# The two-dimensional convolution and whitening kernel: samples of the last two channel groups packed in halves, last-pass loads and covariances one group sooner, and a last pass with full-width evictions, another output layout and stores on two queues

## The chip, the cores and the metric

The kernel runs on one core of one Trainium2 chip. The metric is the device time of one execution in microseconds. Times of before: 909.0 us, the median of three runs (908.66 to 910.16). Engines are named as in the profile: PE (TensorE), DVE (VectorE), ACT (ScalarE), POOL (GpSimd) and SP (SyncE, which issues DMAs).

## The reference

The input is x with shape (4, 64, 256, 256), float32. Layer 0 is a long convolution in two dimensions, computed in the reference by FFTs, whose filter for each channel is a product of a row filter and a column filter. Layer 1 subtracts a mean and whitens the 64 channels.

```python
hx = _implicit_filter(z, Xw1, ...); hy = _implicit_filter(z, Yw1, ...)   # (1, 256, 64)
k = einsum('ijk,imk->ijmk', hx, hy)[0]          # rank one for each channel
y = irfft2(rfft2(x) * rfft2(k) / fft_size)[..., :256, :256] + x * bias[:, None, None]
x1 = transpose(y, (1, 0, 2, 3)).reshape(64, -1)
x1_s = x1[:, ::9]                               # every ninth pixel
mean1 = mean(x1_s); cov = x1_s @ x1_s.T / n + 0.01 * I
out = isqrt_newton_schulz(cov, 5) @ (x1 - mean1)
```

The whitening matrix needs the sampled pixels of all channels and all images, so no output can be written before the whole convolution is done.

## The kernel before, in words

**Start.** Small networks give the filters' taps, which go through DRAM (`g_d`) and come back as Toeplitz matrices (`toep`), one set for each group of 8 channels. Between the small products `busy(n)` issues n plain 128x128 matmuls whose result nobody reads. The last such call is `busy(16)`, ahead of the first half group.

**Main loop.** A step is one channel group g (8 channels, `CG`) of one image n; 32 steps, `steps`. Groups 0 to 5 run over all four images; the last 8 steps alternate groups 6 and 7 for each image, so that an image is complete after every second step. In a step c goes 0, 2, 4, 6. Each `group(first, second)` does the first product for two channels of `first` and, in the same PE sequence, the second product for two channels two positions back in the order (`second`); ACT copies the first product from PSUM to `o1`, DVE adds the bias term to the second product and writes it over x (line 406). Eight PSUM banks turn over, four for each `group`. The order of PE, SP, DVE, ACT and POOL is the program's order (`tc.manual_schedule`), up to the last pass, whose order the tile scheduler sets.

**Packing.** The covariance needs every ninth pixel. `pack_ops` gives 9 DVE operations (`copy_predicated`, line 318) for each step; they copy candidates into `samp[n]`. `store` puts them in the list `todo` when the last pair of channels of a step is stored, and `pack(time)` issues operations until a budget of cost units is used: `pack(2.5)` in each `group`, ahead of `store`. In the last step only the first four channels go this way (9 smaller operations); the others are packed by PE (`pack_by_pe`, line 299).

**Covariance.** `covariance(n)` is 116 small matmuls on `samp[n]` (line 332). For images 0 to 2 it stands in the step of group 7 of the next image, at c == 4; for image 3 after the loop. Then `samp[n]` is free.

**Loads of the last pass.** The convolved images lie in DRAM as `y_d[n]`. A piece is 128 rows (two halves of the image for each of 64 channels) by 4096 pixels, 2 MB; there are 32. `homes` lists 13 buffers that are taken over from the convolution: `e` scratch, `t` Toeplitz sets, `s` sample tiles, `i` x tiles. `early` says after which (step, c) a piece is loaded ahead; nine are. The other four follow after the loop; each waits until its buffer is free. From the 14th piece on, a load waits until the piece 13 places earlier has been stored. All of these loads are issued by SP (line 356).

**Whitening.** `whitening` is a chain of 64x64 products on PE and small DVE and ACT operations, with `spin(n)` (n plain matmuls) between them. It ends with `W` and `shift`.

**Last pass.** For each piece, four times, over 1024 columns: eight matmuls (line 622; each float32 product shows as two matmuls) into two PSUM banks, then two ACT and two DVE operations on 64 partitions by 512 columns each (lines 627 and 630), which add the shift and write over the piece. POOL issues the stores (line 635): whole pieces, and quarters for the first two and the last two pieces.

Of the kernel before, what the change touches and what calls it, by code (L numbers as in the profile page):

```python
# [34 lines left out]
F32 = mybir.dt.float32  # L38
I32 = mybir.dt.int32
AF = mybir.ActivationFunctionType  # L40
ALU = mybir.AluOpType
# [22 lines left out]
def conv_whiten_kernel(ctx: ExitStack, tc: tile.TileContext, a: dict, out: bass.AP):  # L64
# [112 lines left out]
    nc.scalar.dma_start(out=g0_d[CG:], in_=taps[ORDER : ORDER + CG])  # L177
    nc.gpsimd.dma_start(out=g_d, in_=taps)
    nc.gpsimd.tensor_copy(rows, mask[:, NB - 1, 0, :])
    busy(16)  # L180

    def new_toeplitz(g):

# [142 lines left out]
    def covariance(n):  # L326
# [18 lines left out]

    homes = [
        {"t": (tpool, "toep"), "s": (spool, "samp"), "i": (xpool, "in"), "e": (epool, "extra")}[k]
        for k in "eetssiistiits"
    ]

    def load_y(i):
# [19 lines left out]
    for g in range(1, C // CG):  # L371
# [3 lines left out]
            blocks[k // 4, k % 4 * 2] = (g, part)  # L375

    early = {
        (26, 4): 1, (27, 0): 1, (27, 4): 1, (28, 0): 1, (29, 6): 1, (30, 2): 1, (31, 2): 1, (31, 4): 1, (31, 6): 1
    }
    orders = [list(range(L // HP)), list(reversed(range(L // HP)))]  # L380

    def pack(time=math.inf):
        while todo and time > 0:
            cost, op = todo.pop(0)
            op()
            time -= cost

    def group(first, second):

        units = []  # L390
        g1, n1, c1, x1, o1s1 = first
        g2, n2, c2, x2, o1s2 = second
        for u in range(2):
            job2 = (bank(f"p2_{g2}_{n2}_{c2 + u}"), o1s2[u], toep[g2][:, 1, c2 + u, :])
            job1 = (bank(f"p1_{g1}_{n1}_{c1 + u}"), x1[:, c1 + u], toep[g1][:, 0, c1 + u, :])
            units.append((job1, job2))

        toeplitz_products(units, orders[0])
        orders.reverse()
        for u in range(2):  # L400
            o1 = o1pool.tile([P, H2, L], F32, tag="o1", name=f"o1_{g1}_{n1}_{c1 + u}")
            for to, fr in ((slice(0, HP), slice(HP, P)), (slice(HP, P), slice(0, HP))):
                nc.scalar.copy(o1[to], units[u][0][0][fr])  # L403
            o1s1.append(o1)
            ch = g2 * CG + c2 + u
            nc.vector.scalar_tensor_tensor(  # L406
                x2[:, c2 + u], x2[:, c2 + u], bias[:, ch : ch + 1], units[u][1][0],
                ALU.mult, ALU.add,
            )

        pack(2.5)
        store(second)

    def store(second):
        g, n, c, yt, _ = second
        last = (g, n) == steps[-1]
        for b in range(H2):
            row = b * C + g * CG + c
            nc.sync.dma_start(
                out=y_d[n][row : row + 2, :].rearrange("c (p w) -> p c w", w=L),  # L420
                in_=yt[:, c : c + 2, b],
            )
        if last and c == CG // 2 - 2 or not last and c == CG - 2:
            todo.extend(pack_ops(g, n, yt, slice(0, c + 2)))

    spins = []

# [23 lines left out]
    def whitening(i15, ones):  # L451
# [57 lines left out]
        for k in range(1, N_ITER - 1):  # L509
            pq = product(T, T, f"pq{k}")  # L510
            if before is not None:
                next_z(k - 1, before)
            spin(1)
            Q = Qs[k % 2]
            nc.vector.tensor_copy(Q, pq)
            pm = product(Q, M, f"pm_{k}")
            before = T
            if k == 1:
                nc.vector.scalar_tensor_tensor(Z[:, 0:C], Ah, rn_c, one_i15, ALU.mult, ALU.add)
                pzm = product(Z[:, 0:C], mean, "pzm")  # L520
                nc.scalar.copy(Z[:, C : C + 1], pzm)
            if k < N_ITER - 2:
                spin(1)
                T, M = Ts[k % 2], Ms[k % 2]
                nc.vector.scalar_tensor_tensor(T, pm, -0.5, one_i15, ALU.mult, ALU.add)
                nc.vector.tensor_copy(M, pm)
                for _ in range(2):
                    steps_rs.pop(0)()
            else:
                next_z(k, T)  # L530
                spin(1)

                T = place(2 * C, rows=C)
                nc.vector.scalar_tensor_tensor(
                    T.rearrange("p (u c) -> p u c", u=2),
                    pm.unsqueeze(1).to_broadcast([C, 2, C]), -0.5, i15, ALU.mult, ALU.add,
                )
        Z = Zs[(N_ITER - 2) % 2]
        pw = product(T, Z, "pw")
        W = place(C)  # L540
        nc.vector.tensor_scalar(W, pw[:, 0:C], rs, None, ALU.mult)
        shift = const.tile([P, 1], F32, tag="shift", name="shift")
# [4 lines left out]
    with tc.manual_schedule(  # L547
        engines={engines.PE, engines.SP, engines.DVE, engines.Activation, engines.Pool}
    ):
        toep = {0: new_toeplitz(0)}  # L550

        for f, lo, hi in ((0, 0, 2), (0, 2, 4), (0, 4, 6), (1, 0, 2), (0, 6, 8), (1, 2, 4), (1, 4, 8)):
            for half in range(2):
                load_toeplitz(toep[0], 0, f, half, lo, hi, nc.scalar if half else nc.sync)
        for c in range(0, CG, 2):
            load_x(x_tiles[1], *steps[1], c)
        for i, (g, n) in enumerate(steps):
            xt = x_tiles[i % 4]
            for c in range(0, CG, 2):
                item = (g, n, c, xt, [])  # L560
                if g == C // CG - 1 and n > 0 and c == 4:
                    covariance(n - 1)
                if len(pending) == 2:
                    group(item, pending.pop(0))
                else:
                    half_group(item, 0)
                pending.append(item)
                if i == 0 and c == 6:

                    fold = const.tile([P, C], F32, tag="fold", name="fold")  # L570
                    nc.vector.tensor_tensor(fold, ident[:, 0:C], ident[:, C:P], ALU.add)

                    nc.scalar.activation(bf[:, 0:1], samp[0][:, 0, 0, C : C + 1], AF.Sqrt)
                if i == 1 and c < CG - 2:
                    load_pick(c // 2 * 3, c // 2 * 3 + 3)

                if i + 2 < len(steps):
                    load_x(x_tiles[(i + 2) % 4], *steps[i + 2], c)
                if (i, c) in blocks:
                    tg, part = blocks[i, c]  # L580
                    if part == 0:
                        toep[tg] = new_toeplitz(tg)
                    lo = part % 2 * CG // 2
                    load_toeplitz(toep[tg], tg, part // 4, part // 2 % 2, lo, lo + CG // 2)
                for _ in range(early.get((i, c), 0)):
                    load_next()
        g, n, c, yt, _ = pending[0]
        for item in pending:
            half_group(item, 1)
            pack(1.0)  # L590
            store(item)

        pack()
        i15 = place(2 * C, rows=C).rearrange("p (u c) -> p u c", u=2)
        for u in range(2):
            nc.vector.tensor_scalar(i15[:, u], ident[0:C, 0:C], 1.5, None, ALU.mult)
        ones = place(P, rows=C)
        nc.gpsimd.memset(ones, 1.0)  # L598
        for lo in range(CG // 2, CG, 2):
            pack_by_pe(g, n, yt, slice(lo, lo + 2))  # L600
        covariance(NB - 1)
        while len(loaded) < len(homes):
            load_next()
        W, shift = whitening(i15, ones)


    halves = [slice(u * C, (u + 1) * C) for u in range(2)]
    for i, (n, q) in enumerate(pieces):
        yt = loaded.pop(i)
        o = out[n].rearrange("b c f -> (b c) f")[:, q * FP : (q + 1) * FP]  # L610

        part = FP if 1 < i < len(pieces) - 2 else FP // 4
        for w in range(FP // 1024):


            po = [
                psA.tile([P, 512], F32, tag="psA", name=f"po_{n}_{q}_{w}_{u}") for u in range(2)
            ]
            cols = [slice((2 * w + k) * 512, (2 * w + k + 1) * 512) for k in range(2)]
            for k in range(2):  # L620
                for u in range(2):
                    nc.tensor.matmul(  # L622
                        po[u][halves[k]], lhsT=W[halves[u]], rhs=yt[halves[u], cols[k]],
                        start=True, stop=True,
                    )
            for k in range(2):
                nc.scalar.activation(  # L627
                    yt[halves[0], cols[k]], po[0][halves[k]], AF.Identity, bias=shift[halves[k]]
                )
                nc.vector.tensor_scalar(  # L630
                    yt[halves[1], cols[k]], po[1][halves[k]], shift[halves[k]], None, ALU.add
                )
            end = (w + 1) * 1024
            if end % part == 0:
                nc.gpsimd.dma_start(out=o[:, end - part : end], in_=yt[:, end - part : end])  # L635
        if i + len(homes) < len(pieces):
            loaded[i + len(homes)] = load_y(i + len(homes))

# [57 lines left out]
```

## Time and profile before

| | before |
|---|---|
| median of three runs | 909.0 us (908.66 to 910.16) |
| profiled execution, its own time | 907.37 us |
| its span | 905.3 us |
| PE busy | 784.6 us (87%) |
| DVE busy | 656.2 us (72%) |
| ACT busy | 481.5 us (53%) |
| DMA, mean | 285.61 MB, 315 GB/s |
| HBM read, written | 149.35 MB, 134.44 MB |
| line 630, DVE, 64x512 | 256 of 750 ns |
| line 627, ACT, 64x512 | 256 of 683 ns |

The profile divides the span into 40 slices of 22.6 us. PE and its weight load are busy in all of them up to about 620 us; from there on the DMA share is full to nearly the end. The profiled execution took 907.37 us by its own clock, 2.1 us more than the span of its instructions.

### The profile page before, as it was taken

What the parts mean: (1) busy time and instruction counts of PE and PEld (TensorE: products, weight loads), DVE (VectorE), ACT (ScalarE), POOL (GpSimd) and SP (SyncE); (2) the same over time, 40 slices, a digit from 0 to 9 for tenths busy, and PEclk for the clock granted to TensorE, in tenths of its full rate; (3) what the DMA queues carried; (4) which work ended last, traced back from release to release, by engine and by line L of the source; (5) the groups of instructions that cost most, each with busy time, mean ns of one, the idle gap of its engine ahead of it and who ended that gap; (6) DMA issues with size and microseconds to landing.
All of it is one profiled execution on the core that took longest, in us unless ns stands there. A gap on an engine that the chain in (4) does not pass through costs nothing.

```text
span 905.3 us, 28200 instructions
## 1 busy us (share of the span) xinstructions
PE 784.6 (87%) x11892; PEld 630.5 (70%) x11892; DVE 656.2 (72%) x868; ACT 481.5 (53%) x804; POOL 26.4 (3%) x63
## 2 busy tenths in 40 slices
PE   8999999999999999999999999999977777765500
PEld 7999999999999999999999999998411111111100
DVE  3378777877687868776787766767799999996500
ACT  2655555545454545455555544541698888884400
POOL 1000000000000000000000000000100000000010
PEclk9999999999999999999999999999999999996655
DMA  7988779788788788888997899879999999999998
GB/s 215 317 256 263 247 244 273 249 264 247 255 269 262 239 260 270 260 248 256 291 283 233 292 389 341 289 245 384 382 389 428 430 433 429 429 430 431 433 429 340
DMA packets 117496, 285.61 MB, mean 315 GB/s; under 512 B 8987, under 2 KB 91212, under 8 KB 109692
## 3 DMA queue, kind: packets, MB, share of 16 engines
q1 hardware_dynamic: 109676, 215.58, 70.5%
q0 software_dynamic: 6400, 67.31, 17.6%
q8 instruction: 94, 1.54, 0.7%
q10 hardware_dynamic: 1296, 0.93, 0.5%
q14 instruction: 30, 0.25, 0.1%
HBM read 149.35 MB, written 134.44 MB: 313 GB/s over the span
## 4 chain that ended last, share of the span: by engine, by line
PE 68%; DVE 16%; issue 9%; DMA 5%; POOL 0%; ACT 0%; POOLq 0%; DVEq 0%; SPq 0%; ACTq 0%
PE p L219 63%; DVE yi L630 14%; DMA yi<-y_d 3%; PE pc L332 2%; DVE samp L318 1%; DMA out_dram<-yi 1%; PE ph L251 1%; PE po L622 1%; DMA toep<-g_d 0%; POOL out_dram L635 0%; DVE x L288 0%; DVE x L406 0%; ACT yi L627 0%; PE pm L157 0%; PE spin L433 0%
## 5 line engine op out<-in xcount | busy, mean ns | idle before, releaser
L219 PE MATMUL p<-toep,o 64*64 64x64 f32 (+3 forms) x5040 | 578.6, 284 | 0.0
L219 PE MATMUL p<-toep,x 64*64 64x64 f32 (+3 forms) x5040 | 578.4, 284 | 0.1
L219 PEld LDWEIGHTS p<-toep,x 64*128 64x128 f32 (+1 forms) x5040 | 534.6, 166 | 23.9 <-POOLq L235 0.4
L219 PEld LDWEIGHTS p<-toep,o 64*128 64x128 f32 (+1 forms) x5040 | 535.4, 166 | 10.4
L403 ACT COPY o<-p 64x512 f32<-64x512 f32 x504 | 292.2, 580 | 292.9 <-PE p L219 285.3
L318 DVE COPY_PREDICATED samp<-mask,x 128x448 f32<-128x448 int32 (+3 forms) x288 | 281.0, 976 | 6.7
L406 DVE SCALAR_TENSOR_TENSOR x<-x,bias,p 128x512 f32<-128x512 f32 x252 | 177.3, 743 | 138.6 <-PE p L219 138.2
L630 DVE TENSOR_SCALAR yi<-po,shift 64x512 f32<-64x512 f32 x256 | 192.1, 750 | 21.1 <-PE po L622 14.8
L622 PE MATMUL po<-yi,chain 64*64 64x512 f32 x1024 | 149.7, 652 | 61.7 <-DVE yi L630 42.2
L627 ACT ACTIVATE yi<-po,shift 64x512 f32<-64x512 f32 x256 | 174.7, 683 | 37.8 <-PE po L622 30.6
L622 PEld LDWEIGHTS po<-yi,chain 64*64 64x64 f32 x1024 | 34.9, 141 | 175.5 <-DVE yi L630 131.4
L635 POOL DMA_DIRECT2D out_dram<-yi x44 | 23.4, 533 | 254.5 <-DVE yi L630 132.4
L332 PE MATMUL pc<-samp 128*64 128x65 f32 x464 | 16.1, 233 | 2.2 <-ACT samp L308 2.2
L598 POOL MEMSET chain<- 64x128 f32 x1 | 0.2, 198 | 606.0 <-PE ph L251 606.0
L332 PEld LDWEIGHTS pc<-samp 128*64 128x64 f32 x464 | 15.5, 147 | 3.3 <-issue 3.3
L285 DVE COPY o<-ph 64x256 f32<-64x256 f32 x8 | 3.4, 422 | 11.2 <-PE ph L251 11.1
L340 DVE SCALAR_TENSOR_TENSOR cov<-pc,cov 128x65 f32<-128x65 f32 x4 | 0.9, 227 | 13.4 <-PE pc L332 13.4
L251 PE MATMUL ph<-toep,x 64*128 64x192 f32 (+3 forms) x64 | 8.0, 391 | 1.8 <-DMA toep<-g_d 1.8
L285 ACT COPY o<-ph 64x256 f32<-64x256 f32 x8 | 2.9, 366 | 12.1 <-PE ph L251 12.0
L251 PEld LDWEIGHTS ph<-toep,x 64*128 64x128 f32 x64 | 7.2, 234 | 2.5 <-issue 1.5
L299 PE MATMUL pk<-x,pick 128*128 128x56 f32 (+1 forms) x72 | 8.3, 292 | 0.0
L299 PEld LDWEIGHTS pk<-x,pick 128*128 128x128 f32 x72 | 8.1, 192 | 0.1
(93 smaller groups left out, 81.1 us busy)
## 6 DMA issues: line engine op xcount, KB each, us to landing
x<-in_x_dram SPq DMA_DIRECT2D x128, 512.0 KB, 5.5
y_d<-x SPq DMA_DIRECT2D x256, 256.0 KB, 4.0
yi<-y_d SPq DMA_DIRECT2D x32, 2048.0 KB, 14.7
out_dram<-yi POOLq DMA_DIRECT2D x28, 2048.0 KB, 42.8
out_dram<-yi POOLq DMA_DIRECT2D x16, 512.0 KB, 8.5
toep<-g_d SPq DMA_DIRECT2D x28, 256.0 KB, 6.1
toep<-g_d SPq DMA_DIRECT2D x29, 192.0 KB, 6.3
toep<-g_d SPq DMA_DIRECT2D x4, 128.0 KB, 4.0
```

The lines of the kernel that those rows point to most:

```text
L219: mm = nc.tensor.matmul(ps[q : q + w, m, HP * k : L], lhsT=src[parts, k // 2, m * P + q : m * P + q + w], rhs=t[parts, : stop : -1] if k e ...
L251: mm = nc.tensor.matmul(ps[m][:, HP * k : L], lhsT=src[parts, k // 2, m * P : (m + 1) * P], rhs=t[parts, : stop : -1] if k else t[parts, : ...
L285: copy(o1s[u][to, m], ps[fr])
L299: nc.tensor.matmul(pk[:, b, :, 0:nj], lhsT=pick[:, (s - b) % STEP, :], rhs=yt[:, cs, b, s : s + STEP * (nj - 1) + 1 : STEP], start=(s == 0 ...
L318: nc.vector.copy_predicated(dst, m, src)
L332: nc.tensor.matmul(pc[half], lhsT=samp[n][:, b, j, 0:C], rhs=samp[n][:, b, j, :], start=(b == 0 and j < 2), stop=(b == H2 - 1 and j >= NJ ...
L403: nc.scalar.copy(o1[to], units[u][0][0][fr])
L406: nc.vector.scalar_tensor_tensor(x2[:, c2 + u], x2[:, c2 + u], bias[:, ch : ch + 1], units[u][1][0], ALU.mult, ALU.add,)
L622: nc.tensor.matmul(po[u][halves[k]], lhsT=W[halves[u]], rhs=yt[halves[u], cols[k]], start=True, stop=True,)
L627: nc.scalar.activation(yt[halves[0], cols[k]], po[0][halves[k]], AF.Identity, bias=shift[halves[k]])
L630: nc.vector.tensor_scalar(yt[halves[1], cols[k]], po[1][halves[k]], shift[halves[k]], None, ALU.add)
L635: nc.gpsimd.dma_start(out=o[:, end - part : end], in_=yt[:, end - part : end])
```

## The change

The diff has these parts:

- **Start:** `busy(16)` becomes `busy(22)`.
- **Packing:** `store` comes ahead of `pack`, whose budget is now 2.92 units a group and is carried over in `credit`. For groups 6 and 7, in all images, a step's samples are packed in two halves of four channels (9 operations each); the first half is queued after the second pair of channels is stored.
- **Covariances:** those of images 0 to 2 at c == 2 instead of c == 4.
- **Loads ahead:** five of the nine entries of `early` come sooner, by two (one of them four) positions of c, and two entries of `homes` change places.
- **Whitening:** six `spin(1)` become `spin(2)`; `spin(4)` is added ahead of the last covariance and `spin(2)` after the last product; two small operations go from DVE to POOL.
- **Last pass:** ACT and DVE each do one operation on 128 partitions by 512 columns where they did two on 64. For that the output has another layout: the two 64-row halves of a result bank now hold pixels that lie half a piece apart, and a piece is one contiguous block of 2 MB in DRAM. Stores of piece 0 go in four parts, of pieces 1, 30 and 31 in two. SP issues the stores of piece 0 and of pieces 19 to 31; POOL those of pieces 1 to 18.

```diff
-    busy(16)
+    busy(22)
-        for k in "eetssiistiits"
+        for k in "eetssiistitis"
     early = {
-        (26, 4): 1, (27, 0): 1, (27, 4): 1, (28, 0): 1, (29, 6): 1, (30, 2): 1, (31, 2): 1, (31, 4): 1, (31, 6): 1
+        (26, 4): 1, (27, 0): 1, (27, 4): 1, (28, 0): 1, (29, 2): 1, (30, 0): 1, (31, 0): 1, (31, 2): 1, (31, 4): 1
     }
+    credit = [0.0]
     def pack(time=math.inf):
-        while todo and time > 0:
+        credit[0] += time
+        while todo and credit[0] > 0:
             cost, op = todo.pop(0)
             op()
-            time -= cost
+            credit[0] -= cost
+        if not todo:
+            credit[0] = min(credit[0], 0.0)
...
-        pack(2.5)
         store(second)
+        pack(2.92)
...
-        last = (g, n) == steps[-1]
+        halves = g >= C // CG - 2
-        if last and c == CG // 2 - 2 or not last and c == CG - 2:
-            todo.extend(pack_ops(g, n, yt, slice(0, c + 2)))
+        if c == CG - 2 and (g, n) != steps[-1]:
+            todo.extend(pack_ops(g, n, yt, slice(CG // 2 if halves else 0, CG)))
+        elif c == CG // 2 - 2 and halves:
+            todo.extend(pack_ops(g, n, yt, slice(0, CG // 2)))
...
-            spin(1)
+            spin(2)
...
         pw = product(T, Z, "pw")
+        spin(2)
...
-                if g == C // CG - 1 and n > 0 and c == 4:
+                if g == C // CG - 1 and n > 0 and c == 2:
                     covariance(n - 1)
...
-            nc.vector.tensor_scalar(i15[:, u], ident[0:C, 0:C], 1.5, None, ALU.mult)
+            nc.gpsimd.tensor_scalar(i15[:, u], ident[0:C, 0:C], 1.5, None, ALU.mult)
...
+        spin(4)
         covariance(NB - 1)
...
-        o = out[n].rearrange("b c f -> (b c) f")[:, q * FP : (q + 1) * FP]
-        part = FP if 1 < i < len(pieces) - 2 else FP // 4
+        v = yt.rearrange("p (v f) -> p v f", v=2)
+        o = out[n, q].rearrange("p (v f) -> p v f", v=2)
+        part = 512 if i == 0 else 1024 if i == 1 or i > len(pieces) - 3 else 2048
         for w in range(FP // 1024):
+            cols = slice(w * 512, (w + 1) * 512)
...
-                        po[u][halves[k]], lhsT=W[halves[u]], rhs=yt[halves[u], cols[k]],
+                        po[u][halves[k]], lhsT=W[halves[u]], rhs=v[halves[u], k, cols],
...
-            for k in range(2):
-                nc.scalar.activation(
-                    yt[halves[0], cols[k]], po[0][halves[k]], AF.Identity, bias=shift[halves[k]]
-                )
-                nc.vector.tensor_scalar(
-                    yt[halves[1], cols[k]], po[1][halves[k]], shift[halves[k]], None, ALU.add
-                )
-            end = (w + 1) * 1024
+            nc.scalar.activation(v[:, 0, cols], po[0], AF.Identity, bias=shift)
+            nc.vector.tensor_scalar(v[:, 1, cols], po[1], shift, None, ALU.add)
+            end = (w + 1) * 512
             if end % part == 0:
-                nc.gpsimd.dma_start(out=o[:, end - part : end], in_=yt[:, end - part : end])
+                issue = nc.sync if i == 0 or i + len(homes) >= len(pieces) else nc.gpsimd
+                issue.dma_start(out=o[:, :, end - part : end], in_=v[:, :, end - part : end])
...
-    out = nc.dram_tensor("out_0_dram", (NB, H2, C, PIX // H2), F32, kind="ExternalOutput").ap()
+    out = nc.dram_tensor("out_0_dram", (NB, PIX // H2 // FP, P, FP), F32, kind="ExternalOutput").ap()
```

More of the change, by code (lines that the diff above doesn't have):

```diff
@@ L522, in whitening @@
             if k < N_ITER - 2:
-                spin(1)
+                spin(2)
                 T, M = Ts[k % 2], Ms[k % 2]
@@ L530, in whitening @@
                 next_z(k, T)
-                spin(1)
+                spin(2)
                 T = place(2 * C, rows=C)
@@ L539, in whitening @@
         pw = product(T, Z, "pw")
+        spin(2)
         W = place(C)
@@ L618, in conv_whiten_kernel @@
             ]
-            cols = [slice((2 * w + k) * 512, (2 * w + k + 1) * 512) for k in range(2)]
             for k in range(2):
@@ L692 @@
     r = run_bass_kernel_spmd(nc, [arrays], core_ids=[0])
-    y = np.asarray(r.results[0]["out_0_dram"]).reshape(NB, H2, C, PIX // H2)
-    return np.ascontiguousarray(y.transpose(0, 2, 1, 3)).reshape(NB, C, L, L)
+    y = np.asarray(r.results[0]["out_0_dram"]).reshape(NB, PIX // H2 // FP, H2, C, H2, FP // 2)
+    return np.ascontiguousarray(y.transpose(0, 3, 4, 1, 2, 5)).reshape(NB, C, L, L)
```

## The prediction

> **What bounds the kernel now.** I read the 40 slices first, because they show where the bound changes.
>
> ```profile
> DVE  3378777877687868776787766767799999996500
> PEclk9999999999999999999999999999999999996655
> DMA  7988779788788788888997899879999999999998
> GB/s 215 317 256 263 247 244 273 249 264 247 255 269 262 239 260 270 260 248 256 291 283 233 292 389 341 289 245 384 382 389 428 430 433 429 429 430 431 433 429 340
> ```
>
> Up to about 618 us (27 slices) PE is full and DMA is not. From there to the end DMA runs at about 430 GB/s. DVE's nines in the last pass mislead: at the end DVE falls to 0 and DMA goes on, so DVE is ahead of what bounds. The chain of waits names DVE line 630 because it follows the last work back through the stores. I therefore asked for windows around the end of the loop (columns: PE, PEld, DVE, ACT, POOL busy, PE clock, DMA share, GB/s):
>
> ```profile
> 595.00:600.00 5.00, 5.00 (x88) 4.47 (x80) 4.93 (x7) 3.36 (x7) 0.00 (x0) 1.00 0.36 117
> 620.00:645.00 25.00, 21.36 (x251) 18.19 (x254) 14.08 (x46) 3.18 (x15) 0.00 (x0) 0.93 1.01 422
> 645.00:670.00 25.00, 21.47 (x150) 5.39 (x142) 24.23 (x34) 24.31 (x37) 5.00 (x10) 1.00 0.95 371
> 670.00:890.00 220.00, 126.36 (x866) 28.81 (x862) 167.25 (x223) 149.78 (x220) 17.37 (x33) 0.86 1.01 428
> ```
>
> From 670 to 890 nothing can be gained by engines: 428 GB/s in every stretch, reads and writes mixed. There are two soft places: the dips between 645 and 670, and idle DMA in the loop, where too few loads are queued. So the time is: first store, plus the bytes left then over 428 GB/s, plus what DMA loses to gaps. In the order of time, PE ahead of the first store and POOL from it on (start, duration, in brackets the idle time before):
>
> ```profile
> 618.27 8.28 PE L299 MATMUL pk<-x,pick 128*128 128x58 f32 x72
> 628.71 4.93 PE L332 MATMUL pc<-samp 128*64 128x65 f32 x116 [2.16 <-ACT samp L308]
> 643.16 7.47 PE L622 MATMUL po<-yi,chain 64*64 64x512 f32 x57 [0.38 <-DVE chain L541]
> ```
>
> ```profile
> 646.53 0.53 POOL L635 DMA_DIRECT2D out_dram<-yi  x1 [28.36 <-DVE yi L630]
> 663.61 0.53 POOL L635 DMA_DIRECT2D out_dram<-yi  x1 [5.66 <-DVE yi L630]
> 669.79 0.53 POOL L635 DMA_DIRECT2D out_dram<-yi  x1 [5.66 <-ACT yi L627]
> ```
>
> The covariance waits 2.16 us for a copy that waits for DVE's packing (ten operations, 621.21 to 628.07). Whole pieces reach POOL every 6.19 us, 2.1 MB each: 339 GB/s. Until loads come back, that is less than DMA can move; this makes the dips. Last the start of the kernel:
>
> ```profile
> 13.60:17.00 3.40, 1.65 (x11) 1.31 (x13) 0.00 (x0) 0.00 (x0) 0.00 (x0) 1.00 0.89 217
> 17.00:20.40 3.40, 3.40 (x27) 3.35 (x25) 0.46 (x2) 0.66 (x2) 0.00 (x0) 0.50 0.99 213
> ```
>
> PE waits for the first Toeplitz sets 1.33 and 0.45 us; in the next 3.4 us its clock is halved.
>
> **Start, busy(22).** Six more matmuls are 12 records; 32 of them took 3.74 us, so +1.4 us, from 13.58 to about 14.95, where the first half group begins anyway (14.91). They fill the 1.33 us wait. If then the half clock (17.0 to 20.4) goes, PE does in 1.7 us what took 3.4; no wait is recorded in that stretch, and the sets land ahead. I take -1.5 us, bounds 0 (the 0.45 us wait alone still halves it) and -1.7. The loop is PE-bound, so all later times move with it.
>
> **Packing in halves.** Groups 6 and 7 cost DVE 18 operations a step for 9. The rows:
>
> ```profile
> L318 DVE COPY_PREDICATED samp<-mask,x 128x448 f32<-128x448 int32 x155 | 150.9, 973 | 4.2
> L318 DVE COPY_PREDICATED samp<-mask,x 128x224 f32<-128x224 int32 x5 | 3.1, 611 | 0.2
> L406 DVE SCALAR_TENSOR_TENSOR x<-x,bias,p 128x512 f32<-128x512 f32 x252 | 177.3, 743 | 138.6 <-PE p L219 138.2
> ```
>
> A group then has 4.5 operations of 0.62 us and two of line 406, 1.40 us in the timeline together: 4.2 us. Stores of successive groups leave SP at 608.98 and 613.36, 4.4 us apart. So it fits by 0.2 us, and three covariances (3.71 us of PE each) give DVE slack. I cost it at nothing; the cover is PE, and PSUM banks are reused only a group later. Above 0.66 us for a half the group would be DVE-bound, and above 0.75 (17.5 us of four groups, plus 1.6 of covariances, less 5.6, over 18) their slack would be used up too; that is a rival below. The 2.92 budget in groups 0 to 5 leaves three full operations a group as now, at nothing.
>
> **End of the loop.** By the order of instructions DVE has seven half operations left after its last line 288 where it had ten: 4.5 us, done near 625, before PE's packing ends (626.55). The copy then ends near 627.0 and `spin(4)` (8 records; 14 took 1.83 us) at 627.65: the covariance starts 1.06 us sooner. PE has no gap, so I expect no half clock from 628: 3.71 us as in the loop (599.27) for 4.93, -1.2. In the whitening each `spin(1)` starts 0.42 us ahead of the product behind it, six times alike, so PE is the limit there and six more spins cost 6 x 0.22 = +1.35 us. The spin after `pw` ends as `W` does: nothing. POOL's two operations (0.28 us on DVE) are done during the packing. Sum -0.9 us, bounds -2.3 (spins free) and +0.3 (half clock stays).
>
> The Trainium skill, "TensorE: Matmul & The Clock Gate", section "HAM oscillation", says that PE must not idle for more than about 3.4 us, so waits of 1.33 and 2.16 us should be harmless and the added matmuls only a cost. By that rule both clock terms (1.5 and 1.2) would be nothing and the sum below about 2.7 us smaller. This trace shows the clock at 0.50 after each of the two, and I go by it.
>
> **First store.** Now 3.37 us lie between the first matmul (643.16) and POOL's issue. The first ACT operation starts 1.19 us after the first matmul, DVE 1.25; then one operation of 0.75 and the issue: 2.05 us. -1.3 us, bounds -0.8 and -1.7, since SP's issue to first byte is not shown beside POOL's for such a store.
>
> **Eviction at full width.** 128 DVE operations go, and 128 of ACT. Line 406 shows that 128 partitions by 512 columns take DVE 743 ns, as 64 take it 750. A piece costs ACT and DVE 3.0 us; PE's matmuls start in fours 0.42 us apart before DVE holds them (644.07, 644.50, 644.92), so eight records take 0.84 us and a piece 3.4. Supply is then 617 GB/s, over DMA's 428, and the dips go: 645 to 670 moved 371 x 25 = 9.3 MB, which takes 21.7 us at 428, so -3.3 us. Bounds 0 and -3.4. The rest of the 100 us of DVE time saved lies beside DMA and is worth nothing.
>
> **Loads sooner.** With 13 buffers at most 13 pieces can be in before the first store lands. Adding up GB/s from 645 to the end gives 108.0 MB; 67.1 of it is output, so 19.5 pieces were unread and 12.5 read. Sooner loads can fill the last half piece, 2.4 us at most, and only if the first store would otherwise wait in the queue behind it. That condition makes the terms above count: by 642 all 13 must be in. Loads go 4.4 us sooner, the last is freed by the covariance 3.8 us sooner; so yes, nearly. No gain of its own. Moved past them on SP are `x` loads of the last steps, needed 30 us later, and `y_d` stores, which nobody awaits in the loop. Covariances at c == 2 need packing that ended two groups earlier: nothing.
>
> **Queues and layout.** SP's store of piece 19 stands ahead of its load of piece 31, and later stores behind that load, which waits for store 18. POOL's stores are in flight meanwhile: nothing, or at most one piece, 4.9 us, if the queue runs dry. Piece 0 in runs of 2 KB: between the 428 here and the 306 GB/s at full share that the loop's small transfers show (257 at 0.84), 0 to +2.0 us; nearer 4 KB, so +0.3. Contiguous output at nothing, as strided rows already reach 428. The tail after the last byte, 1 us either way.
>
> **Sum.** -1.5 - 0.9 - 1.3 - 3.3 + 0.3 = -6.7: span 898.6, the execution's own time 907.37 - 6.7 = 900.7. The median of before is 1.63 above its profiled execution, so 902.3. A measurement can tell about 0.2% (1.8 us) from no change.
>
> **Rivals.** (1) *Terms fail, the end stays DMA's* (0.20): the half clock at the start stays, and half of the dips come back because loads and stores now share SP's queue: +1.5 +1.7, so 905.5. For it: 0.45 us of wait remains in that window. (2) *No change* (0.06): the 13 buffers are not in when the first store is ready, the stores queue behind loads, dips move to where piece 19 changes queue: -6.7 + 1.5 + 4.9 = about 908.7. Against it: 600 to 620 has idle DMA for the loads. (3) *Slower* (0.07): the half operations cost more than 0.75 us each and DVE bounds steps 24 to 30. Were one as dear as a full one (0.973), a step would take 18 x 0.973 + 5.6 = 23.1 us against 17.5 for PE plus 1.6 for covariances: seven steps x 4.0 = +28, 930. It turns the sign from 0.82 us on: 7 x 18 x 0.07 = +8.8 us against the -6.7. Against it: nine such operations at 611 and 627 ns. (4) *Forecast* (0.67), its own range 899 to 904.5.
>
> **Range and chances.** 898.8 to 906.5 holds most of the forecast and of (1). Faster 0.87, same 0.06, slower 0.07.
>
> **What would show it.** Right: clock 1.00 from 17 to 20.4 and from 628; the first matmul of line 622's successor near 640.8 and the first store from SP near 642.8; 425 GB/s or more within a few us of it, with no dip; DVE near half busy in the last pass; span less the first issue near 255.8 us against 258.8. Wrong: idle PE gaps in steps 24 to 31 that end on DVE, DMA under 400 GB/s after 650, or a stretch without transfers where stores pass from POOL to SP.

## The result, and the profile after

| | before | after |
|---|---|---|
| median, run side by side | 909.58 us (908.66 to 911.18) | 902.97 us (902.13 to 903.93) |
| profiled execution, its own time / span | 907.37 / 905.3 us | 903.93 / 902.1 us |
| PE busy | 784.6 us | 781.2 us |
| DVE busy | 656.2 us | 581.5 us |
| ACT busy | 481.5 us | 395.5 us |

The changed kernel takes 0.9934 of the time of before, interval 0.9917 to 0.9952: 6.6 us less, where 6.7 had been forecast. Run again beside other kernels it took 902.45 us, a ratio of 0.9926 (0.9912 to 0.9940). The sign and the size are settled. The terms of the sum are another matter, and most of what follows is about them.

One caution first. The profiled execution of before (907.37) lies below its median, that of after (903.93) is the slowest of its four. The two profiles are therefore only 3.4 us apart, and a sum over them can explain 3.4 us of the 6.6, no more. That is why I read the profiles of several kernels side by side below.

The 40 slices of after:

```profile
DVE  3487778877888778877888877877688332233200
PEclk9999999999999999999999999999999766866755
DMA  7988889798788888888997899979999999999998
GB/s 209 327 262 252 242 261 271 234 273 251 247 263 261 244 264 259 258 250 267 293 275 241 285 351 356 335 237 390 375 401 429 430 432 432 429 434 430 430 430 355
```

The shape is that of before: PE's part up to about 618 us, then DMA at 430 GB/s. DVE has dropped from nines to twos and threes in the last pass, at no change of the GB/s there: that saving lay beside DMA, as the prediction held. In the slices of steps 24 to 31 (about the 21st to the 28th) DVE stays at 7 or 8 tenths.

The windows of after (PE, PEld, DVE, ACT, POOL busy, PE clock, DMA share, GB/s):

```profile
13.60:17.00 3.40, 2.47 (x23) 2.31 (x23) 0.00 (x0) 0.00 (x0) 0.00 (x0) 1.00 0.91 189
17.00:20.40 3.40, 3.40 (x41) 3.19 (x39) 0.93 (x3) 1.08 (x3) 0.00 (x0) 1.00 1.01 243
...
640.00:645.00 5.00, 5.00 (x44) 3.21 (x47) 1.43 (x6) 1.30 (x4) 0.00 (x0) 1.00 0.95 403
645.00:650.00 5.00, 5.00 (x52) 1.79 (x48) 4.43 (x7) 4.02 (x7) 0.00 (x0) 1.00 0.70 260
...
655.00:660.00 5.00, 5.00 (x53) 1.71 (x48) 4.36 (x7) 3.97 (x7) 1.08 (x2) 1.00 1.08 369
...
645.00:670.00 25.00, 25.00 (x240) 8.98 (x236) 21.97 (x30) 19.99 (x30) 4.12 (x7) 1.00 0.95 360
670.00:890.00 220.00, 116.84 (x780) 38.36 (x768) 73.61 (x99) 67.37 (x98) 6.41 (x12) 0.73 1.01 430
```

The clock is 1.00 from 17.0 to 20.4 (0.50 before). From 645 to 670, where I had expected the dips to go, DMA moves 360 GB/s: less than the 371 of before. From 645 to 650 its share is 0.70: for a part of that stretch nothing is there to be moved.

In the order of time, PE at the end of the loop (start, duration):

```profile
619.32 8.28 PE L300 MATMUL pk<-x,pick 128*128 128x58 f32 x72
627.42 1.10 PE L442 MATMUL spin<-ident 128*128 128x128 f32 x8
628.45 3.71 PE L333 MATMUL pc<-samp 128*64 128x65 f32 x116
...
643.18 7.10 PE L635 MATMUL po<-yi,chain 64*64 64x512 f32 x64
```

```profile
645.57 3.51 SPq L645 DMA_DIRECT2D out_dram<-yi  x4
```

```profile
650.03 0.73 POOL L645 DMA_DIRECT2D out_dram<-yi  x1 [29.80 <-ACT yi L639]
651.69 0.69 POOL L645 DMA_DIRECT2D out_dram<-yi  x1 [0.92 <-DVE yi L640]
655.12 0.55 POOL L645 DMA_DIRECT2D out_dram<-yi  x1 [2.74 <-DVE yi L640]
658.55 0.53 POOL L645 DMA_DIRECT2D out_dram<-yi  x1 [2.88 <-DVE yi L640]
```

The covariance now starts 0.85 us behind PE's packing (2.16 before) and takes 3.71 us (4.93 before). The first store is SP's and comes at 645.57, 0.96 us sooner than POOL's at 646.53. Whole pieces then reach POOL every 3.43 us (6.19 before): 2.1 MB in 3.43 us is 611 GB/s of supply, where 617 was forecast.

The group of line 640 says that a full-width eviction costs DVE what a half-width one did (751 ns, 750 before) at half the count:

```profile
L640 DVE TENSOR_SCALAR yi<-po,shift 128x512 f32<-128x512 f32 x128 | 96.1, 751 | 109.0 <-PE po L635 100.7
```

Last, a small thing that is not in before, from the waits:

```profile
PEld p L220 <- issue: 1.5, 3, 0.8
...
PE p L220 <- issue: 0.8, 2, 0.5
```

In the loop PE stops a few times for no semaphore: the profile calls it "issue". Before shows no such wait at line 219.

The profiles cut at the events that the prediction named. Each row is a stretch of the span, in us, with the difference to before; e1, g4 and k2 are kernels of the next section:

| stretch | before | after | e1 | g4 | k2 |
|---|---|---|---|---|---|
| to the first full group | 23.07 | −0.81 | −0.98 | −1.00 | −1.08 |
| loop, to PE's packing | 595.20 | +1.86 | −0.55 | −0.85 | −0.35 |
| PE's packing, then wait for the copy (spins in it) | 8.28 + 2.16 | −1.31 | −1.30 | −1.80 | −1.80 |
| last covariance | 4.93 | −1.22 | −1.22 | −1.24 | −1.24 |
| whitening, `pd` to first `po` | 9.20 | +1.50 | +1.50 | +1.18 | 0.00 |
| first `po` to first store | 3.37 | −0.98 | −0.98 | −0.09 | +0.01 |
| first store to the end | 258.77 | −2.19 | −1.92 | −1.64 | +0.34 |
| span | 905.3 | −3.15 | −5.46 | −5.45 | −4.14 |

### The profile page after: what moved, and what is told of

The parts are those of the page before. It is cut to its first block, busy times and chain, and to the rows that moved or that the text cites. A ratio compares the mean times of both kernels' runs of the same rounds, so it can differ in the third digit from the quotient of the medians.

```text
span 902.1 us, 28046 instructions
## 1 busy us (share of the span) xinstructions
PE 781.2 (87%) x11928; PEld 647.5 (72%) x11928; DVE 581.5 (64%) x801; ACT 395.5 (44%) x676; POOL 14.5 (2%) x40
## 4 chain that ended last, share of the span: by engine, by line
PE 74%; DMA 11%; another core or an unknown queue 7%; DVE 0%; issue 0%; SPq 0%; ACT 0%; POOLq 0%; DVEq 0%
PE p L220 64%; DMA out_dram<-yi 5%; DMA yi<-y_d 5%; PE po L635 4%; PE pc L333 2%; PE ph L252 1%; PE pk L300 1%; PE spin L442 1%; DMA toep<-g_d 0%; PE busy L152 0%; PE pm L158 0%; SPq L357 0%; DMA scratch<-in_zw_dram 0%; DVE yi L640 0%
## 5 line engine op out<-in xcount | busy, mean ns | idle before, releaser
L220 PEld LDWEIGHTS p<-toep,o 64*128 64x128 f32 (+1 forms) x5040 | 536.7, 166 | 10.7 <-issue 0.2
L319 DVE COPY_PREDICATED samp<-mask,x 128x464 f32<-128x464 int32 (+3 forms) x351 | 297.2, 847 | 9.8 <-DVE x L412 0.2
L412 DVE SCALAR_TENSOR_TENSOR x<-x,bias,p 128x512 f32<-128x512 f32 x252 | 179.8, 744 | 121.3 <-PE p L220 117.3
L635 PE MATMUL po<-yi,chain 64*64 64x512 f32 x1024 | 143.7, 720 | 60.4 <-DMA yi<-y_d 60.4
L640 DVE TENSOR_SCALAR yi<-po,shift 128x512 f32<-128x512 f32 x128 | 96.1, 751 | 109.0 <-PE po L635 100.7
L635 PEld LDWEIGHTS po<-yi,chain 64*64 64x64 f32 x1024 | 48.0, 162 | 155.2 <-issue 150.5
L639 ACT ACTIVATE yi<-po,shift 128x512 f32<-128x512 f32 x128 | 88.0, 687 | 116.7 <-PE po L635 116.0
L645 POOL DMA_DIRECT2D out_dram<-yi x19 | 10.5, 554 | 130.5 <-DMA out_dram<-yi 55.1
L152 PE MATMUL busy<-idle 128*128 128x128 f32 x64 | 9.4, 307 | 0.0
L152 PEld LDWEIGHTS busy<-idle 128*128 128x128 f32 x64 | 8.9, 222 | 0.2 <-issue 0.2
L442 PE MATMUL spin<-ident 128*128 128x128 f32 x50 | 7.9, 292 | 0.0
L286 ACT COPY o<-ph 64x256 f32<-64x256 f32 x8 | 2.9, 368 | 10.7 <-DMA toep<-g_d 9.2
```

The source lines that it names most:

```text
L152: nc.tensor.matmul(p, lhsT=idle[:, 0:P], rhs=idle[:, P : 2 * P], start=True, stop=True)
L220: mm = nc.tensor.matmul(ps[q : q + w, m, HP * k : L], lhsT=src[parts, k // 2, m * P + q : m * P + q + w], rhs=t[parts, : stop : -1] if k e ...
L319: nc.vector.copy_predicated(dst, m, src)
L412: nc.vector.scalar_tensor_tensor(x2[:, c2 + u], x2[:, c2 + u], bias[:, ch : ch + 1], units[u][1][0], ALU.mult, ALU.add,)
L442: nc.tensor.matmul(p, lhsT=ident, rhs=ident, start=True, stop=True)
L635: nc.tensor.matmul(po[u][halves[k]], lhsT=W[halves[u]], rhs=v[halves[u], k, cols], start=True, stop=True,)
```

## The experiments

Each ratio is against runs of before on the same chip in the same session (medians of before 908.42 for the kernels whose names begin with e, 909.57 for h and g, 908.45 for k).

**Is it the six matmuls at the start?** e1 is after with

```diff
-    busy(22)
+    busy(16)
```

> The changed kernel with busy(16) at the start, as before. The theory of the prediction (the half clock from 17 to 20.4 us costs 1.5 us, and the loop passes it on whole) expects +1.5 us over the changed kernel, about 904.5, and a clock of 0.50 in one 3.4 us stretch after the wait for the first Toeplitz sets. The rival (what is won at the start is lost in the loop, since the changed trace was 0.8 us ahead after the first group and 1.1 us behind at its end) expects the same time as the changed kernel within 0.5 us.

Measured: 901.96 us, ratio 0.9930 (0.9914 to 0.9946), the same as after. Its windows at the start:

```profile
13.60:17.00 3.40, 1.25 (x12) 1.08 (x12) 0.00 (x0) 0.00 (x0) 0.00 (x0) 1.00 0.87 164
17.00:20.40 3.40, 3.40 (x40) 3.17 (x38) 1.09 (x3) 1.24 (x4) 0.00 (x0) 1.00 1.11 275
```

PE is busy for 1.25 us of the first stretch, less than the 1.65 of before, and the clock behind it is 1.00 all the same. So the half clock of before's profile was not the price of too few matmuls. g4, k2, k3 and k4, also with `busy(16)`, show none there either; before does, and so does k1, at 0.50 from 16.40 to 19.82.

The traces show what sets the two apart. In each of the 14 traces all moments at which the granted clock changes lie whole multiples of 3.413 us from one another (in before 17.01, 20.43, 628.00 and 631.41), and where this grid lies in the span differs from execution to execution. PE waits 2.15 us for the first Toeplitz sets in e1 and 2.24 us in k1, nearly the same. The windows of their grids, first two of e1, then two of k1:

```profile
11.98:15.40 3.42, 2.19 (x20) 1.99 (x18) 0.00 (x0) 0.00 (x0) 0.47 (x2) 1.00 0.57 137
15.40:18.81 3.41, 2.49 (x27) 2.39 (x27) 0.00 (x0) 0.00 (x0) 0.00 (x0) 1.00 1.06 241
```

```profile
12.99:16.40 3.41, 1.19 (x11) 1.01 (x10) 0.00 (x0) 0.00 (x0) 0.00 (x0) 1.00 0.83 193
16.40:19.82 3.42, 3.40 (x18) 3.37 (x19) 0.00 (x0) 0.00 (x0) 0.00 (x0) 0.50 1.03 229
```

In e1 an edge of the grid cuts the wait in two, and PE is busy for more than 2 us of either window. In k1 the wait falls into one window, of which PE is busy for 1.19 us, and the next window runs at half the clock; in before that window (13.60 to 17.01) has 1.66 us of PE. So nearly the same wait runs into the half clock in one execution and not in another. With `busy(22)` the wait is 0.93 us in after, and none of the seven profiles with `busy(22)` has the half clock there, against two of seven with `busy(16)`.

**Are the other added matmuls worth their time?** e4 is after with the six `spin(2)` back at `spin(1)` and none behind `pw`; g4 takes away all the clock matmuls:

```diff
-    busy(22)
+    busy(16)
...
-            spin(2)
+            spin(1)
...
-        spin(2)
         W = place(C)
...
-        spin(4)
         covariance(NB - 1)
```

> The changed kernel with spin(1) in the six places of the whitening and no spin after the last product; spin(4) ahead of the covariance stays. The theory (PE is the limit in the whitening, each spin costs 0.22 us there, and the first store sets the end) expects the first matmul of the last pass 1.4 us sooner and -1.4 us, about 901.5. The rival (DMA is still reading pieces until about 645 us, so a sooner first store only queues) expects -0.5 us to 0.

> The changed kernel with every clock-keeping matmul as before: busy(16), six spin(1), no spin(4) and none after the last product. Theory: these matmuls buy no mean time, they only keep half-clock stretches of 3.4 or 6.8 us out; without them PE's half clock shows in the profile between 620 and 645 us in some executions, the times spread more, and the median is 0 to +1 us. Rival (the prediction's): without the half clock's cover the covariance takes 4.9 us for 3.7 and the start 1.5 us more, but the whitening is 1.35 us shorter: +1.4 us, about 904.

Measured: e4 902.05 us, 0.9933 (0.9914 to 0.9951); g4 901.87 us, 0.9923 (0.9904 to 0.9941). Neither differs from after. The windows of g4:

```profile
636.30:643.10 6.80, 6.42 (x32) 3.24 (x34) 1.53 (x4) 1.36 (x4) 0.00 (x0) 0.50 0.86 366
...
645.00:670.00 25.00, 25.00 (x236) 8.34 (x232) 21.87 (x30) 20.05 (x30) 4.10 (x7) 1.00 1.00 387
```

In g4, without the spins, the clock is halved for 6.8 us, in the second half of the chain and into the first evictions (e4: the same at 637.8). That gives back what the shorter chain saves: 10.4 us from `pd` to `po` instead of 10.7 (0.3 us sooner, where e4's expectation had 1.4), and then 3.28 us to the first store instead of 2.39. This too is a chance: before and k2, with the same chain, run it at 1.00, while k1, k3 and k4 show a half clock that begins within it. With the matmuls that stretch is at 1.00 in all seven profiles that have them. It is a draw in the median; g4 spreads more, from 900.52 to 905.09, than after in the same session, from 902.20 to 903.54. The covariance of g4 takes 3.69 us without `spin(4)` (k2 and k4 the same), so the full clock there does not need it where the wait for the copy is short.

**The packing, with loads and covariances.** e2 is after with all of these as before (`pack(2.5)` ahead of `store`, whole steps, the old `early` and `homes`, covariances at c == 4). k2 is before with the new packing alone:

```diff
+    credit = [0.0]
     def pack(time=math.inf):
...
-        pack(2.5)
         store(second)
+        pack(2.92)
...
-        last = (g, n) == steps[-1]
+        halves = g >= C // CG - 2
```

> The changed kernel with the packing, the places of the covariances, the early loads and the homes of before; start, whitening and last pass stay changed. The theory of the prediction gives these parts no gain of their own in loads, only about 1 us at the end of the loop (the copy that waits for DVE): +1 us, about 904. The rival (the loads fill DMA that is idle between 595 and 620 us, where the two traces differ by 1.0 MB left at 620, and the end is set by bytes) expects +2.4 us or more, about 905.5 to 907, with as many bytes left at 620 us as before.

> The kernel before with the packing of after alone (store ahead of pack, budget 2.92 carried over, groups 6 and 7 in halves). Theory: DVE ends its packing ahead of PE, so the last covariance starts 0.4 us behind PE's packing and not 2.2, and the first store and the end come 1 to 1.8 us sooner. Rival (DVE falls behind in the last eight steps, since a half operation costs more than 0.66 us there): PE waits for DVE in those steps and the kernel is 1 us or more slower.

Measured: e2 904.41 us, 0.9959 (0.9945 to 0.9973). k2 904.69 us, 0.9954 (0.9940 to 0.9969): 3.8 us from the packing alone. e2 lies 2.0 us above after (902.45) and 2.4 us above e1 of its own session, nearer the second of its expectations; it does not tell packing from loads. PE in k2, in the order of time:

```profile
616.84 8.28 PE L299 MATMUL pk<-x,pick 128*128 128x58 f32 x72
625.47 3.69 PE L332 MATMUL pc<-samp 128*64 128x65 f32 x116 [0.36 <-issue]
```

The wait of 2.16 us is down to 0.36, and the covariance runs at full clock. These two make 3.0 us; the rest of k2's 4.1 us of span lies at the start (1.08, where the profile of before has its half clock) and in the loop (0.35).

**The loads and covariances.** g2 is after with the old places of both; k3 is before with the new places and the old packing:

```diff
-        for k in "eetssiistiits"
+        for k in "eetssiistitis"
...
-        (26, 4): 1, (27, 0): 1, (27, 4): 1, (28, 0): 1, (29, 6): 1, (30, 2): 1, (31, 2): 1, (31, 4): 1, (31, 6): 1
+        (26, 4): 1, (27, 0): 1, (27, 4): 1, (28, 0): 1, (29, 2): 1, (30, 0): 1, (31, 0): 1, (31, 2): 1, (31, 4): 1
...
-                if g == C // CG - 1 and n > 0 and c == 4:
+                if g == C // CG - 1 and n > 0 and c == 2:
```

> The changed kernel with early loads, homes and covariances at their places of before; the packing in halves and all else stay changed. It splits the 2.4 us that the packing and the loads gave together. Theory now: the 13 buffers are full before the first store in either case, so sooner loads give at most 0.5 us and the rest came from DVE being done sooner at the end of the loop; the time stays within 0.7 us of the changed kernel. Rival (bytes): fewer bytes are moved by 620 us, and the whole 2 us come back, about 904.5.

> The kernel before with the early loads, the homes and the places of the covariances of after alone. Theory: the buffers are full before the first store in either case, so what is moved sooner before 620 us (about 1.5 MB) is given back as idle DMA between 640 and the first store; 0 to -0.9 us. Rival (bytes): -2 us or more.

Measured: g2 903.34 us, 0.9932 (0.9917 to 0.9948), beside 902.45 and 0.9926 of after: the intervals cover each other. The windows of g2:

```profile
640.00:645.00 5.00, 5.00 (x40) 3.81 (x43) 1.25 (x7) 0.74 (x4) 0.00 (x0) 1.00 1.01 433
645.00:650.00 5.00, 5.00 (x52) 1.73 (x48) 3.96 (x6) 3.68 (x6) 0.00 (x0) 1.00 0.97 401
```

With the old loads DMA is full right up to the first store; with the new ones (0.70 in after) it has nothing left to load shortly before. Sooner loads move idle DMA from the loop to the time ahead of the first store.

k3 was a surprise: 925.42 us, 1.0182 (1.0163 to 1.0202), 17 us slower than before. One line of its waits and three windows, each behind one of the waits:

```profile
PE pc L332 <- DVE samp L318: 12.7, 3, 4.2
```

```profile
516.10:519.50 3.40, 3.40 (x71) 3.40 (x67) 0.00 (x0) 0.00 (x0) 0.00 (x0) 0.50 1.09 394
560.50:567.30 6.80, 5.14 (x95) 5.17 (x97) 1.48 (x2) 0.00 (x0) 0.00 (x0) 0.50 0.51 174
608.30:615.10 6.80, 5.92 (x109) 5.95 (x111) 0.73 (x1) 0.00 (x0) 0.00 (x0) 0.50 0.83 314
```

At c == 2 the packing of the image before is not done when a whole step is packed at once; PE stands 4.2 us before each of three covariances and then runs at half the clock. 12.7 us of waits and up to half of 17.0 us at half clock are more than the 17 us that PE's packing starts later than in before (635.22 against 618.27). The covariances at c == 2 need packing that is done sooner; of the kernels here, those with the packing in halves have it.

**The last pass.** e3 is after with before's last pass, layout and POOL stores; k1 is before with the new ones. The core of k1:

```diff
-                nc.scalar.activation(
-                    yt[halves[0], cols[k]], po[0][halves[k]], AF.Identity, bias=shift[halves[k]]
-                )
...
+            nc.scalar.activation(v[:, 0, cols], po[0], AF.Identity, bias=shift)
+            nc.vector.tensor_scalar(v[:, 1, cols], po[1], shift, None, ALU.add)
```

> The changed kernel with the last pass of before: evictions of 64 partitions, the old layout, all stores on POOL. The theory of the prediction (first store 1.3 us sooner, dips of 3.3 us gone) expects +4.3 us, about 907. The rival (the dips only changed place: the changed trace moves 360 GB/s from 645 to 670 us where before moved 371) expects +1 us or less, about 903 to 904.

> The kernel before with the last pass of after alone (full-width evictions, new layout, stores on SP and POOL). The theory of the prediction for this part is -4.3 us (first store 1.3 sooner, dips of 3.3 gone, small runs +0.3). The theory after the first experiments: -3.2 us, of which 1.0 is the sooner first store and 1.9 the stretch from the first store to the end, while 645 to 670 us still moves less than 400 GB/s.

Measured: e3 905.84 us, 0.9969 (0.9957 to 0.9981), so the new last pass is worth about 3.4 us to the changed kernel (905.84 less 902.45). Alone it is worth 1.6 us: k1 906.87 us, 0.9981 (0.9965 to 0.9996), with a wide spread (903.25 to 910.61). PE in k1 shows why this end is worse than it need be:

```profile
618.67 8.28 PE L299 MATMUL pk<-x,pick 128*128 128x58 f32 x72
629.31 5.95 PE L332 MATMUL pc<-samp 128*64 128x65 f32 x116 [2.37 <-ACT samp L308]
```

The wait for the copy is there, the clock falls behind it, and the covariance takes 5.95 us in this execution.

**Which queue stores.** g1 is after with every store on POOL:

```diff
-                issue = nc.sync if i == 0 or i + len(homes) >= len(pieces) else nc.gpsimd
+                issue = nc.gpsimd
```

> The changed kernel with all stores of the last pass issued by POOL. If the store queue matters (SP brings the first store sooner and takes the later stores out of POOL's queue), the first packets come up to 1 us later and the end is 1 to 2 us later, about 904. If only bytes and the moment of the first store count, the time stays within 0.5 us.

Measured: 903.70 us, 0.9935 (0.9920 to 0.9949), 1.25 us above after in the same session, inside the intervals, so it does not tell the two expectations apart. From the first matmul to the first store it takes 2.62 us (2.39 from SP).

**The changed kernel again**, to have it beside the g kernels:

> The changed kernel itself, timed beside the next three on the same chip. Both theories expect 902 to 903 us, 0.7% below before.

Measured: 902.45 us (902.20 to 903.54), 0.9926 (0.9912 to 0.9940).

**A better version?** The stores of piece 0 are rows of 2 KB and cost some bandwidth. k4 is g4 with piece 0 in two parts of 4 KB rows and piece 1 whole:

```diff
-        part = 512 if i == 0 else 1024 if i == 1 or i > len(pieces) - 3 else 2048
+        part = 1024 if i == 0 or i > len(pieces) - 3 else 2048
```

> A candidate: the changed kernel with the clock-keeping matmuls as before and with piece 0 stored in two parts (runs of 4 KB, where it had 2 KB in four parts) and piece 1 whole. If the small runs of the first two pieces make the 370 GB/s between 648 and 665 us, that stretch rises to over 400 GB/s and the time is 1 us under the changed kernel, about 901 to 901.5. If the later first store (one more step of 0.86 us) takes that back, 902 to 902.5.

Measured: 902.51 us, 0.9924 (0.9908 to 0.9939): no better. The first store comes 4.72 us behind the first matmul instead of 3.28, and the last stretch is 0.8 us shorter. From 648 to 665 us k4 moves 386 GB/s, not over 400, and g4 moves 386 as well. What the last stretch gains, the later start takes. No kernel here beats the changed one by more than its interval.

## Why the prediction was right, and where its terms were not

**What bounds the kernel: right.** From 670 to 890 all profiles move 428 to 430 GB/s (but for k3, whose last pass begins some 20 us later: 424). So one figure judges all that lies ahead: the megabytes still to move at 645 us, over 428 GB/s, and what the rest loses against that rate. Summed from the GB/s of the traces:

| | MB left at 645 | end at 428 GB/s | span | lost |
|---|---|---|---|---|
| before | 108.00 | 897.3 | 905.3 | 8.0 |
| after | 107.22 | 895.5 | 902.1 | 6.6 |
| after, again (h0) | 107.15 | 895.3 | 901.8 | 6.5 |
| e1 | 106.82 | 894.6 | 899.8 | 5.2 |
| g2 | 108.87 | 899.4 | 905.0 | 5.6 |

Of the 3.2 us between the two profiles, 1.8 are bytes moved sooner and 1.4 are smaller losses in the last pass.

**Start, −1.5: failed.** I took the 1.33 us wait of PE for the cause of the half clock. e1 has no more matmuls there than before, a longer wait (2.15 us) and no half clock; k1, with the same lines, has it. What counts is how much of a wait falls into one window of the grid. The Trainium skill, "TensorE: Matmul & The Clock Gate", section "What's actually happening", says that the activity window of 3413 ns is free-running, so that what a run sees depends on the phase in which its work falls. The grid of 3.413 us in these traces, the stretches at 0.50 of one or two of its windows, and the same code at 1.00 in e1 and at 0.50 in k1 agree with that. Its section on oscillation, which the prediction weighed, speaks of idle time above about 3.4 us; at the start and in the chain no wait is that long, in k1 one of 2.24 us was enough, and in g4 the profile has PE busy for 3.34 of the 3.42 us ahead of the half clock. So the row was right that short waits can be followed by the half clock, and wrong as a price: it is a chance, not a cost paid in each run. The median time shows no gain from `busy(22)` (902.45 and 902.97 against 901.96).

It may even cost something. Seven of the profiles have `busy(22)`, and all seven show "issue" stops of PE or of its weight loads in the loop; the seven with `busy(16)`, before among them, show none of that name. Their loops, from the first full group to PE's packing, last 595.1 to 598.3 us and 594.3 to 595.2 us (k3 left out, whose loop has the waits shown). In after the loop is 1.86 us longer than in before and 2.4 us longer than in e1, which eats what the start gains; the stops that the profile names add up to 0.8 us of PE and 1.5 us of its weight loads. What they are was not settled: the profile names no releaser, and e1, which differs from after in nothing but `busy`, was profiled once. There is a lead: in nine places of the loops two matmuls start more than 0.55 us apart (the waits of k3 left out), all with `busy(22)`, and each time a packet of the DMA queue that the profile calls "q8 instruction" had started 1.4 to 2.0 us ahead of that gap. Such packets come every few us in all kernels, so why only these kernels stop is not shown.

**End of the loop, −0.9: right in its parts, the price of the spins included.** The copy waits for DVE's packing; the wait is 1.31 us shorter (1.06 forecast), the covariance at full clock 1.22 us shorter (1.2), the spins cost 1.50 us (1.35). What failed is the need for `spin(4)`: the prediction let it hold the covariance back from 627.0 to 627.65 so that PE has no gap, but k2 and g4 start the covariance at 0.36 us instead of 0.85, and have the full clock without it.

**First store, −1.3: measured −0.98**, 2.39 us behind the first matmul instead of 2.05. The chain is the one forecast; at half clock (g4) nearly all of this gain is gone.

**Dips gone, −3.3: the step that failed most.** The supply was forecast right (611 GB/s), but 645 to 670 moves 360 GB/s, below the 371 of before. I had held that the dips were want of stores. Two other things make them now. First the 13 buffers are full and DMA idles until the first store is issued (share 0.70 from 645 to 650). Then comes a stretch in which DMA is full and yet slow: 369 GB/s from 655 to 660 at a share of 1.08. In the trace of after, 2 KB packets of piece 0 run alone from 647 to 652, at 88 ns each and 375 to 389 GB/s; when the loads come back, a 16 KB packet of a load takes 657 ns (655 to 660) and 735 ns (660 to 665) on average, against 612 ns later. In before it takes 750 and 776 ns in the same stretches, so this is not the new rows' doing alone; what lengthens the packets is not shown. So the stretch from first store to end gained 2.0 to 2.2 us (256.8 and 256.6 against 258.8), where the forecast's 255.8 asked for 3.0. In the medians the new last pass is worth 3.4 us to the changed kernel (e3), 2.9 by the two profiles: 1.0 up to the first store and 1.9 behind it, of the 4.3 forecast. The rows of 2 KB, put at +0.3, are part of this: by the packet times they cost about 0.7 us (an estimate: 1024 packets of 88 ns, where an eighth of a 16 KB packet takes 76, over 16 engines). k4 shows that larger ones alone do not bring it back.

**Loads sooner, "no gain of its own": right**, with g2 0.9 us slower inside the intervals. The reason given is not borne out, though: I held that by 642 all 13 "must be in" for the other terms to count. g2 does as well inside the intervals with DMA loading until the first store.

**Packing in halves, "nothing": failed on the low side.** The fit on DVE was right: from the timeline of after, seven half operations take 4.55 us (0.65 each), two bias operations 1.40, so a group needs 4.5 x 0.65 + 1.40 = 4.3 us of 4.4, and PE waits for DVE nowhere in the steps concerned. The gain was booked under the end of the loop, at −2.3 without the spins; k2 gains 3.8 us in the median. And **covariances at c == 2, "nothing"** holds only with it: k3 puts 17 us on the missing condition, which I named (packing ended two groups earlier) without pricing it.

**The rivals.** (1), half of it came true: the dips stayed in part, but the cause was not SP's shared queue, since g1 with POOL alone is no faster (380 GB/s from 645 to 670, 903.70 us). Its other half, a half clock at the start, is not in the profile of after. (2) fell with the result. (3) did not occur: the half operations cost 0.65 us, below the 0.75 from which DVE would bound; k3 shows what a wait on packing would have cost.

**Why the number held.** That it held to 0.1 us is luck: the start and the dips, 4.8 us of the 6.7, gave no sure gain and about 2 us, and two errors met. The sum gave 900.7 us for the profiled execution of after, which took 903.93: 3.2 us too little, by the start and the loop (−1.5 forecast, +1.05 measured) and by the last pass (about 1 us), with the end of the loop as forecast. To this I added the 1.63 us by which before's median lies above its profile; after's median lies 0.96 us below its own. e1, the same kernel but for `busy`, has a profile (901.63) near its median (901.96) and is the fairer test: −5.7 us of its own time against the −6.7. Alone, the parts give −1.6 (k1) and −3.8 (k2), and the loads and covariances +17; together −6.6. So the parts do not add up one by one. What stays open: the spread of before (905.30 to 911.69 over all sessions), which the mean granted clock of its executions does not follow, and so the half of the gain that the two profiles do not show.

## What to carry to other kernels

A clock that is halved in one profile may be an accident of phase: see how the waits lie on the grid on which the clock changes, and look at the same stretch in a second execution, or in a kernel that leaves it untouched, before matmuls are added to mend it. Where a transfer-bound stage follows an engine-bound one, count the bytes that are left at the border; work ahead of it is worth the time by which the first store comes sooner, and sooner loads showed no gain here, where the buffers were full before that store. Before a consumer is moved ahead, price the condition under which its producer is done: here that price was 17 us, and a change of granularity in the producer paid for it.

## What the runs showed of the hardware

- In each trace the granted clock changes only on a grid of 3.413 us. Up to the last 50 us the half clock comes in stretches of one or two windows, behind waits of 4.2 us (k3), of 2.2 to 2.4 us (before, k1) and in a chain whose waits are near 0.5 us (g4). The same wait of 2.2 us at the start halves the clock where it falls into one window (k1) and not where an edge cuts it (e1).
- Where loads of 16 KB packets come back behind and beside stores in rows of 2 and 4 KB, the loads' packets lengthen from 612 ns to 657 and 735 ns (after) or 750 and 776 ns (before). A 4 KB packet of the last stores takes 159 ns, one in the stretch from 652 to 661 of after 190 ns on average, one of 2 KB 88 ns. DMA's share is full then at a lower rate (369 GB/s at 1.08 in after).
- Mixed reads and writes of one core in large rows hold 428 to 430 GB/s for 220 us, whether POOL alone issues the stores (before, g1) or SP and POOL do (after).
- PE or its weight loads stop for 0.2 to 0.9 us at a time in the loop with no releaser in all seven profiles with `busy(22)`, at changing places (83 and 520 us in after), and in none of the seven with `busy(16)`; the nine longest gaps begin 1.4 to 2.0 us behind the start of a packet of the queue "q8 instruction".
